# A fused attention and top-1 expert kernel: another order of the same units, and the fills of ones moved from VectorE to GpSimd

## The chip, the cores and the metric

The kernel runs on one core of one Trainium2 chip. The metric is the device time of one execution in microseconds; the time of a kernel is the median of several executions. A profile is one execution taken by the hardware profiler.

## The reference

The input x has 16 batches of 256 tokens with 128 features, 4096 tokens in all. The output is x plus two blocks that both read the layer-normalized x:

```python
xn = layernorm(x)                                  # over 128 features
# linear attention: 16 heads of 8, 64 random features each
q, k, v = xn @ Wq + bq, xn @ Wk + bk, xn @ Wv + bv
qp = relu(q . rw) + 1e-6;  kp = relu(k . rw) + 1e-6
attn = (qp @ (kp^T v)) / (qp @ sum_s(kp) + 1e-6) @ Wo + bo
# experts: 8, hidden width 512; each token goes to its best one
probs = softmax(xn @ wr + br);  gate = p1 / (p1 + p2)
ffn = gate * (gelu(xn @ w1[e] + b1[e]) @ w2[e] + b2[e])    # e = argmax
out = x + attn + ffn
```

All of it is in float32.

## The kernel before

The work is cut into small named units, and a string, `ORDER` (lines 66 to 116), lists them; line 814 runs through it and emits each. Line 137 fixes the order of TensorE (PE), VectorE (DVE), ScalarE (ACT) and SyncE (SP, which issues the plain DMAs) to that list. GpSimd (POOL) is not in line 137: its order is chosen when the program is built, from the same list and the dependences. Each engine works through its own instructions in order and waits by semaphores. A unit's name has its kind, then its number, then in some kinds the engine: `a` for ScalarE, `v` for VectorE.

**Head.** SP loads x in eight pieces of two batches, h = 0 to 7 (256 KB each, line 150), and two packs of constants. GpSimd and VectorE set up constants; among them VectorE fills with ones the upper half of every group of 32 columns of four tiles `va_c`, one for each chunk of four batches (line 192). These columns make the attention's denominator come out of the same products as its numerator. Then for every piece h:

- `st` (VectorE, line 285, two of them), `vr` (L294), `rs` (GpSimd, L299, the power -1/2), `nm` (L304): statistics; `xn` normalizes four tiles of 128 tokens (L311 on ScalarE or L313 on VectorE).
- `xd` (SP, L321) stores them in DRAM, in rows that the experts' gathers read.
- `tp` (PE, L327) turns the four tiles, `ev` copies them to xnT, `pv` (PE, L341) makes values and router logits; `lg` (L345) and `va` (L351) add the biases, `va` into the lower half of the groups of `va_c`.

For every chunk c: `c0` to `c6` (VectorE, L377 to L383) pick the best expert and the two best logits, `ct` (PE, L394) counts, `g0` to `g3` make the gate, `g4` (SP, L408) stores it beside the rows of xn. Then once: `ra` to `rl` (VectorE, L440 to L457) give every token a slot in 39 tiles of 128 tokens sorted by expert; `e0` to `e2` the expert of each tile; `hh` and `lo` (L475 to L477) compare, `iv0` and `iv1` (PE, L484, 16 products each) invert the map, and `s0` (L496) writes the token table that the gathers read.

**Attention.** For every pair of batches: `pj` (PE, L514) projects keys and queries, `pe` adds the biases (L521 on ScalarE, L523 on VectorE), `pq` (PE, L539) and `qf` (L548, or L555 and L557) make query features. For every batch, named in hexadecimal 0 to f: `pk` (PE, L581), `kf` (ACT, L592) key features, `kv` (PE, L607) keys by values, `mk`, `tk`, `nd` (L619, L630, L270), `at` (PE, L648), `a0` to `a5` (VectorE, L659 to L685) the quotient, `pw` (PE, L693) the output product, `ow` (L695) and `bo` (L697) the adds into x.

**Experts.** For every tile s = 00 to 38: `gx` (GpSimd, L716) gathers 128 rows from DRAM by an indirect DMA, `wl` (SP, L729) loads 578 KB of weights of the tile's expert, `fi` (PE, L734) turns, `xc` copies, `fu` (PE, L747) is the first product, `ht` (ACT, L754, four) the gelu, `gy` (L766) bias times gate, `fd` (PE, L775) the second product, `fy` (L783) the sum, `sc` (GpSimd, L790) scatters the 128 rows to DRAM by another indirect DMA. There are five weight buffers, three of which first hold tables of the routing (`iota_h`, `low` twice), seven buffers for gathered rows and six for results. A gather waits until the tile four before it has been copied out (line 723).

**End.** `ae` (GpSimd, L805) adds the rows of one chunk from DRAM into x by an accumulating DMA, after all scatters; `so` (SP, L700) stores the batches. PSUM is shared by three pools: two buffers for `pv`, `pj`, `pq`, `pk`; three for the small products; one for `ph` and the routing's.

Of the kernel before, what the change touches and what calls it, by code (L numbers as in the profile page):

```python
# [25 lines left out]
Q = 32  # L26
# [11 lines left out]
NCHUNK = B // CHUNK_B  # L38
# [25 lines left out]


ORDER = """
st00 st01 vr0 st10 st11 vr1 rs0 nm0 xn00v xn02v xn03a rs1 xn01v nm1 tp0 xn10v xn11v xn12v st20 xn13a tp1 st21
ev0a vr2 st30 st31 rs2 pv0 vr3 st40 pj0 nm2 xd1 xd0 va0 lg0 ev1a st41 vr4 rs3 xn20a rs4 nm3 xn22v st50 xn30v
xn31v st60 st51 pj1 vr5 xn32v xn33v xn23a pe00a nm4 xn21a pe01a pe11a tp2 pv1 st61 pe10v rs5 ev2a xn40a st70
xn43a nm5 lg1 xn41v xn50a va1 xn52v vr6 c00 tp3 pv2 va2 c01 ev3a xn51a lg2 rs6 xn42a pv3 nm6 tp4 va3 lg3 xn60a  # L70
pk0 xn63v st71 c02 ev4v vr7 c10 c03 xn53a xn61a xn62a c11 c12 tp5 rs7 c13 c14 kf00a kf01a ev5v nm7 tp6 xn70v
xn72a xn73a xn71v c04 c15 c05 c16 pv4 c06 g01 lg4 g00 g10 va4 pv5 ev6a tp7 va5 lg5 pv6 c20 bo1 g11 ev7a pv7 g21
ct0 c21 c22 c23 lg6 va6 g20 ct1 lg7 va7 pq00 c24 c30 c31 g31 c32 c25 g30 ct2 xd4 xd7 c26 c33 c34 qf000a qf000b
xd5 g02 qf001v c35 xd3 ct3 ra rb c36 rc g03 g12 g22 g13 kv0 rd re g23 pq01 rf mk00 e0 qf011a qf011b mk01 xd2 g33
g32 qf010v g40 g41 xd6 g42 rg tk0 e1 rh ri e2 rj g43 rk hh00 rl hh10 lo1 hh01 nd0a lo0 pk1 at0 hh11 kf10a kf11a
pj2 kv1 pe20a mk10 mk11 pe21a pk2 iv0 kf20a wl00 kf21a iv1 s0 a00 s1 bo3 wl01 tk1 pk3 nd1a kv2 mk20 at1 kf30a
kf31a gx00 fi00 gy00v s2 mk21 a01 pq10 xc00a qf100v kv3 fu00 ht000 ht001 wl02 qf101v bo4 gx01 gx02 mk30 ht002
ht003 mk31 gx03 wl03 tk2 fi01 xc01v pq11 nd2a qf110v a10 gy01v qf111v a20 fi02 fu01 xc02a ht010 wl04 ht011 ht012
gy02v ht013 fi03 tk3 fd00 fy00 fu02 xc03a ht020 a30 a40 gy03v a11 pj3 ht021 ht022 nd3a ht023 gx04 fi04 pe31a
xc04a fd01 gx05 pe30v fy01 a21 fu03 ht030 ht031 pk4 ht032 ht033 gx06 fd02 a50 gy04v bo7 bo2 gx07 fu04 fy02 wl05  # L80
bo0 fi05 wl06 ht040 ht041 xc05v pw0 ht042 ht043 gx08 kf40a fd03 sc00 ow0 kf41a fd04 fu05 gy05v fy03 fi06 xc06a
fi07 sc01 gx09 ht050 pk5 fy04 ht051 kv4 ht052 xc07a wl07 ht053 kf50a at2 fu06 kf51a pk6 fi08 ht060 ht061 wl08
ht062 bo6 gy06v a31 a02 mk40 mk41 xc08v ht063 fd05 kf60a fu07 fy05 gy07v tk4 gx10 gx11 kf61a wl09 sc02 fi09 fd06
ht070 ht071 ht072 ht073 a41 fu08 nd4a fi10 pq20 fy06 ht080 xc09a ht081 ht082 a51 ht083 fi11 pw1 fu09 ht090 ht091
gy08v xc10v ht092 wl10 xc11v qf200v ow1 fd07 ht093 sc03 sc04 sc06 gx12 gx13 qf201v fd08 fu10 fd09 wl11 wl12 fy07
fy08 gy09v gx14 a12 fy09 ht100 ht101 ht102 ht103 sc05 fi12 xc12a pq21 kv5 qf210v at3 a22 pj4 fu11 ht110 ht111
ht112 a32 a42 ht113 gx15 sc08 a52 a03 mk50 wl13 pw2 qf211v mk51 ow2 fi13 sc07 gy10v gy11v pe40a gy12v xc13v
pe41a fd10 fu12 ht120 ht121 fd11 fi14 fy10 bo5 fy11 a13 xc14a ht122 gx16 fi15 pq30 ht123 xc15v qf300v gy13v fd12
fu13 fy12 qf301v wl14 gy14v tk5 at4 gx17 ht130 a23 kv6 pq31 ht131 ht132 ht133 nd5a fu14 fi16 ht140 ht141 ht142
sc10 ht143 bo9 a04 mk60 fd13 sc09 a33 mk61 a43 tk6 a14 a24 wl15 fu15 nd6a ht150 wl16 ht151 xc16v gy15v qf311v  # L90
qf310v fd14 a53 fy13 ht152 gx18 ht153 a34 bo8 gy16v fy14 pk7 pw3 fi17 kf70a wl17 ow3 fu16 fi18 pj5 wl18 ht160
ht161 ht162 ht163 xc17v fu17 fd15 sc12 pe51a kf71a at5 a05 fy15 a15 ht170 xc18a kv7 a25 boa mk70 sc13 sc11 gy17v
ht171 ht172 pe50a gx19 ht173 gx20 wl19 pk8 fu18 fi19 ht180 mk71 gx21 gy18v xc19v a44 fi20 fd16 fd17 ht181 ht182
ht183 wl20 sc15 xc20a kf80a kf81a gy19v a54 fy16 fy17 fu19 pw4 gx22 sc14 gx23 fd18 ht190 ht191 ow4 ht192 ht193
fi21 wl21 fu20 fy18 wl22 fd19 a35 fi22 xc21v gy20v xc22v a45 fy19 pq40 ht200 ht201 qf400v ht202 at6 ht203 a06
qf401v kv8 fi23 fu21 fd20 xc23v a55 fy20 sc16 gx24 mk80 gy21v ht210 ht211 mk81 pq41 ht212 ht213 fu22 ht220 ht221
tk7 ht222 ht223 nd7a qf410v pw5 fd21 gx25 ow5 wl23 fy21 qf411v fi24 fu23 wl24 fi25 wl25 at7 pq50 ht230 sc17 gx26
sc18 gx27 ht231 ht232 ht233 xc24v bob a16 a07 a26 gy22v fu24 xc25a a36 a46 a17 tk8 wl26 gx28 sc21 fd22 fd23
qf500v a27 gy23v fy22 sc19 nd8a ht240 ht241 ht242 qf501v fy23 a56 wl27 gy24v ht243 fi26 xc26v fu25 fi27 fd24
pq51 xc27a ht250 fy24 qf511v gy25v ht251 ht252 ht253 fu26 wl28 fi28 ht260 xc28v qf510v fd25 pw6 ht261 ht262  # L100
ht263 gx29 sc20 fy25 ow6 fu27 gy26v a37 fd26 gx30 fy26 ht270 pk9 ht271 ht272 ht273 gx31 sc23 sc22 at8 kf90a gx32
kf91a gy27v a08 fu28 fi29 wl29 wl30 ht280 xc29a wl31 pka fi30 ht281 gx33 sc24 xc30v ht282 ht283 fi31 fd27 fd28
xc31a kfa0a kfa1a pj6 fu29 a47 pe60v fy27 kv9 kva ht290 pe61a ht291 pkb ht292 a18 ht293 fu30 ht300 wl32 gy28v
sc26 sc25 mk90 fy28 a28 gy29v mk91 mka0 ht301 ht302 mka1 fd29 ht303 a38 a48 a57 a58 pw7 pw8 ow7 fy29 ow8 fu31
fi32 xc32v fi33 tk9 fd30 kfb0a kfb1a ht310 ht311 gx34 sc28 ht312 ht313 nd9a xc33v wl33 fu32 ht320 ht321 ht322
ht323 wl34 at9 kvb gx35 sc27 gy30v fy30 mkb0 gy31v a09 pq60 tka a19 gy32v a29 fu33 ht330 ndaa mkb1 a39 fi34
xc34a fd31 boc fd32 fi35 qf600v ht331 ht332 fy31 ht333 xc35v fy32 qf601v gy33v wl35 fu34 ht340 ht341 a49 gx36
ata sc30 ht342 ht343 gy34v bod pq61 qf610v qf611v fu35 fi36 fd33 pj7 a0a ht350 gx37 xc36v ht351 ht352 fi37 wl36
ht353 gx38 sc29 fu36 pe70a xc37a ht360 ht361 gy35v pe71v fy33 ht362 ht363 fd34 fy34 fd35 fi38 wl37 fy35 gy36v
a1a fu37 wl38 ht370 pkc ht371 sc31 sc32 a2a xc38v a3a ht372 ht373 kfc0a a59 fd36 kfc1a fu38 sc35 ht380 bof ht381  # L110
ht382 a4a fd37 sc34 ht383 pkd pw9 boe a5a gy37v fy36 fy37 fd38 ow9 gy38v kfd0a tkb pwa kfd1a sc36 fy38 sc37 sc33
pke kvc owa mkc0 ndba mkc1 atb kvd kfe0a kfe1a sc38 mkd0 a0b a1b tkc pkf a2b mkd1 ndca atc a3b a4b kff0a a5b a0c
a1c a2c kve mke0 a3c kff1a pq70 tkd ndda pwb a4c mke1 ae1 ae2 ae0 ae3 atd kvf a5c qf700v so5 qf701v a0d pq71 so8
so0 owb a1d mkf0 a2d mkf1 sob qf710v qf711v a3d tke so3 so7 so2 a4d tkf pwc ndea a5d owc ndfa so9 so6 soa ate
a0e pwd owd a1e atf a2e a3e a0f so1 so4 soc a4e a1f a5e a2f pwe a3f a4f sod a5f owe soe pwf owf sof
"""


# [1 line left out]
def attn_plus_top1_moe(ctx: ExitStack, tc: tile.TileContext, x, cpack, wpack, out):  # L120
    nc = tc.nc
# [26 lines left out]
    for h in range(NH):  # L148
        c, i = h // 2, 2 * (h % 2)
# [39 lines left out]
    vaug = []  # L189
    for c in range(NCHUNK):  # L190
        va_c = const.tile([P, CT, NPAIR, Q], F32, name=f"va_{c}")
        nc.vector.memset(va_c[:, :, :, Q // 2 :], 1.0)  # L192
        vaug.append(va_c)
    ones = const.tile([P, P], F16, name="ones")
    nc.vector.memset(ones, 1.0)
# [63 lines left out]
    units = {}  # L259
# [8 lines left out]

    def copy(eng, out, in_):
        return nc.scalar.copy(out, in_) if eng == "a" else nc.vector.tensor_copy(out, in_)  # L270


    st, var, rstd, nmr, xns, xnT, pts, pvs = {}, {}, {}, {}, {}, {}, {}, {}
# [2 lines left out]
    def layernorm(h):  # L276
# [52 lines left out]
        def turned(eng):  # L329
            if c not in xnT:  # L330
                xnT[c] = xnp.tile([P, CT, P], F32, tag="xnT", name="xnT", bufs=4)
            copy(eng, xnT[c][:, g : g + 4, :], pts.pop(h))
# [31 lines left out]
    lg2 = route.tile([P, NT, E], F32, name="lg2")  # L364
# [203 lines left out]
    def batch(b):  # L568
# [63 lines left out]
        def turned(eng):  # L632
            nds[b] = work.tile([P, 2, 4, Q], F32, name="nd")
            copy(eng, nds[b].rearrange("p r q c -> p r (q c)"), pns[b])
# [75 lines left out]
    def expert_tile(s):  # L710
# [25 lines left out]
        def turned(eng):  # L736
            xTs[s] = work3.tile([P, P], F32, name="xT")
            copied[s] = copy(eng, xTs[s], pxs[s])
# [126 lines left out]
```

## Time and profile before

| | |
|---|---|
| median of 9 runs | 220.77 us (218.89 to 221.9) |
| the profiled execution | 222.7 us, its span 221.0 us |
| TensorE busy | 197.0 us (89%) |
| VectorE busy | 148.1 us (67%) |
| ScalarE busy | 111.1 us (50%) |
| GpSimd busy | 90.7 us (41%) |
| mean granted TensorE clock | 0.96 |

Times in the views are microseconds from the start of the span, those of single instructions means in ns. A view of waits names what ended an engine's idle time, by semaphore events; where the named engine had long been done it was another. The chain of waits goes back from the last instruction to what released it, step by step.

### The profile page before, as it was taken

The page shows a single profiled execution, that of the slowest core. Times are in us where ns is not written, and L with a number is a line of the kernel's source. Part 1 is how long each engine was busy: PE and PEld are TensorE (multiplying, and loading weights), DVE is VectorE, ACT ScalarE, POOL GpSimd, SP SyncE. Part 2 cuts the span into 40 slices and gives each one's busy share as a digit, 9 for nine tenths or more (in the row PEclk, how much of TensorE's full clock was granted, in tenths as well). Part 3 has the DMA queues.
Part 4 walks back from the last instruction along what each step waited for, and adds up shares of the span by engine and source line. Part 5 has one row for each costly group of instructions (what it writes and reads, how often), then busy time and mean ns, then how long its engine had stood idle before and what let it go on. Part 6 is the DMA issues. An engine that isn't in the chain of part 4 may idle for free.

```text
span 221.0 us, 5940 instructions
## 1 busy us (share of the span) xinstructions
PE 197.0 (89%) x2207; PEld 156.4 (71%) x2207; DVE 148.1 (67%) x437; ACT 111.1 (50%) x275; POOL 90.7 (41%) x104
## 2 busy tenths in 40 slices
PE   0299886994999999999999999999999999999834
PEld 0167764573787988978787989898788878876522
DVE  5999999921774534696863577975163796439973
ACT  6158747543255785424456724436648345854100
POOL 3353100024135747456353676377356153543000
PEclk9999999978599999999999999999999999999995
DMA  6940198795026857677574596489646463109982
GB/s 165 309 98 23 38 174 56 73 333 185 12 44 215 259 170 235 183 244 220 176 237 129 153 328 212 134 242 316 189 149 183 126 232 125 49 15 191 219 281 71
DMA packets 21870, 37.53 MB, mean 170 GB/s; under 512 B 6641, under 2 KB 14962, under 8 KB 21842
## 3 DMA queue, kind: packets, MB, share of 16 engines
q1 hardware_dynamic: 18770, 29.93, 46.1%
q0 software_dynamic: 3072, 7.23, 13.7%
q8 instruction: 17, 0.28, 0.5%
q14 instruction: 11, 0.09, 0.1%
HBM read 30.39 MB, written 6.77 MB: 168 GB/s over the span
## 4 chain that ended last, share of the span: by engine, by line
PE 60%; DVE 16%; DMA 13%; issue 5%; POOL 3%; ACT 1%; SPq 1%; POOLq 0%; DVEq 0%
PE ph L747 16%; PE py L775 15%; PE pq L539 6%; DMA x<-yd 6%; PE pp L514 4%; PE pk L581 4%; PE pkv L607 4%; PE pa L648 4%; DMA xg<-xd,token 3%; PE pw L693 3%; DMA w<-in_wpack_dram 3%; PE pt_x L734 2%; DVE va L351 2%; DVE va L192 2%; DVE xn L313 1%
## 5 line engine op out<-in xcount | busy, mean ns | idle before, releaser
L754 ACT ACTIVATE hT<-ph,w 128x128 f32<-128x128 f32 x156 | 45.9, 374 | 54.7 <-issue 40.2
L716 POOL DMA_INDIRECT xg<-xd,token x39 | 38.3, 982 | 65.0 <-DMA w<-in_wpack_dram 22.9
L790 POOL DMA_INDIRECT yd<-y,row x39 | 38.8, 994 | 28.1 <-DVE y L783 16.7
L747 PE MATMUL ph<-xT,w 128*128 128x128 f32 x312 | 43.7, 284 | 0.1
L747 PEld LDWEIGHTS ph<-xT,w 128*128 128x128 f32 x312 | 39.0, 195 | 6.2 <-issue 5.0
L775 PE MATMUL py<-w,hT 128*128 128x128 f32 x312 | 40.6, 277 | 0.1
L548 DVE TENSOR_SCALAR qpT<-pq 128x1024 f32<-128x1024 f32 x30 | 36.0, 1215 | 5.0 <-PE pq L539 5.0
L775 PEld LDWEIGHTS py<-w,hT 128*128 128x128 f32 x312 | 37.4, 192 | 1.7 <-issue 0.6
L592 ACT ACTIVATE kp<-pk 128x1024 f32<-128x1024 f32 x32 | 31.3, 1032 | 8.4 <-PE pk L581 6.6
L783 DVE SCALAR_TENSOR_TENSOR y<-py,xg,y 128x128 f32<-128x128 f32 x39 | 13.5, 346 | 12.5 <-PE py L775 12.2
L581 PE MATMUL pk<-cw,kT 32*128 32x256 f32 x256 | 20.4, 417 | 1.1 <-DVE qpT L548 0.9
L539 PE MATMUL pq<-qT,cw 32*128 32x256 f32 x256 | 20.2, 417 | 0.3 <-DVE lg L345 0.3
L648 PE MATMUL pa<-qpT,nd 128*32 128x256 f32 x256 | 17.7, 384 | 1.7 <-DVE x L695 1.1
L607 PE MATMUL pkv<-kp,va 128*32 128x129 f32 x512 | 18.4, 290 | 0.0
L607 PEld LDWEIGHTS pkv<-kp,va 128*32 128x32 f32 x512 | 14.9, 116 | 4.7 <-issue 3.1
L659 DVE STREAM_TRANSPOSE at<-pa 128x512 f32<-128x512 f32 x16 | 11.3, 704 | 9.6 <-PE pa L648 9.6
L619 DVE SCALAR_TENSOR_TENSOR kvm<-pkv,hmask 128x128 f32<-128x128 f32 x32 | 10.3, 337 | 8.6 <-PE pkv L607 8.6
L581 PEld LDWEIGHTS pk<-cw,kT 32*128 32x128 f32 x256 | 12.6, 192 | 4.6 <-issue 1.9
L539 PEld LDWEIGHTS pq<-qT,cw 32*128 32x128 f32 x256 | 12.7, 192 | 4.4 <-issue 3.1
L514 PE MATMUL pp<-xnT,cw 128*128 128x512 f32 x32 | 15.1, 599 | 0.1
L327 PE MATMUL pt<-ident,xn 128*128 128x128 f32 x32 | 5.7, 314 | 9.7 <-DVE xn L313 9.7
L299 POOL TENSOR_TENSOR rstd<-var,mhalf 128x4 f32<-128x4 f32 x8 | 8.1, 1017 | 14.3 <-DVE var L294 8.6
(108 smaller groups left out, 236.8 us busy)
## 6 DMA issues: line engine op xcount, KB each, us to landing
w<-in_wpack_dram SPq DMA_DIRECT2D x39, 578.0 KB, 3.8
x<-in_x_dram SPq DMA_DIRECT2D x8, 256.0 KB, 5.1
xd<-xn SPq DMA_DIRECT2D x8, 256.0 KB, 7.3
x<-yd POOLq DMA_DIRECT2D x4, 512.0 KB, 5.2
out_dram<-x SPq DMA_DIRECT2D x16, 128.0 KB, 2.2
xg<-xd,token POOLq DMA_INDIRECT x39, 3.6
yd<-y,row POOLq DMA_INDIRECT x39, 4.2
cw<-in_cpack_dram SPq DMA_DIRECT2D x1, 321.0 KB
```

The costliest lines, as they stand in the source:

```text
L514: nc.tensor.matmul(pps[k][:, i], cst(w), rhs, start=True, stop=True)
L539: nc.tensor.matmul(pqs[k, i][g // 2][:, g % 2, cols], cst("rwf")[rows, i * P : (i + 1) * P], qT[rows, cols], start=True, stop=True,)
L548: nc.vector.tensor_scalar(feats[k][:, i, 2 * g : 2 * g + 2, :], pqs[k, i][g], 0.0, EPS, ALU.max, ALU.add)
L581: nc.tensor.matmul(pks[b][g // 2][:, 2 * (g % 2) : 2 * (g % 2) + 2, t, :], kT[rows, 2 * (b % 2) + t, :], cst("rwf")[rows], start=True, sto ...
L592: nc.scalar.activation(o, i, AF.Relu)
L607: nc.tensor.matmul(pkvs[b][Q * q : Q * q + Q, r, :], vaug[c][:, 2 * bl + t, j, :], kp[:, t, j, :], start=(t == 0), stop=(t == 1),)
L648: nc.tensor.matmul(pas[b][Q * q : Q * q + Q, r, :], nds[b][:, r, q, :], feats[b // 2][:, j % 2, j // 2, cols], start=True, stop=True,)
L716: ins = nc.gpsimd.indirect_dma_start(out=xgs[s], out_offset=None, in_=xd[:, :], in_offset=bass.IndirectOffsetOnAxis(ap=rt["token"][:, s : ...
L747: nc.tensor.matmul(phs[s][:, i, :], ws[s][:, W1O + i * P : W1O + (i + 1) * P], xTs[s], start=True, stop=True)
L754: nc.scalar.activation(hTs[s][:, i, :], phs[s][:, i, :], AF.Gelu, bias=ws[s][:, B1O + i : B1O + i + 1])
L775: nc.tensor.matmul(pys[s], hTs[s][:, i, :], ws[s][:, W2O + i * P : W2O + (i + 1) * P], start=(i == 0), stop=(i == NC - 1),)
L790: ins = nc.gpsimd.indirect_dma_start(out=yd[:, :], out_offset=bass.IndirectOffsetOnAxis(ap=rt["row"][:, s : s + 1], axis=0), in_=ys[s], in ...
```

## The change

The same units are emitted in another order, over the whole list. The four fills of ones become four new units, `vm0` to `vm3`, on GpSimd, one for each chunk. Some units change engine: VectorE has 13 of the 32 `xn` where it had 16 and none of the eight `ev` where it had two, seven of the 16 `pe` (was four) and 20 of the 39 `xc` (was 22). In the list, the fills stand behind `rs6` (vm0), `gx02` (vm1), `sc11` (vm2) and before `gx35` (vm3). The stores of xn go `xd0 xd1 xd4 xd5 xd2 xd3 xd7 xd6` where they went `xd1 xd0 xd4 xd7 xd5 xd3 xd2`, then xd6 between the gates. Ahead of the first expert tile's `fi00`, TensorE has no `pk3`, `at0`, `at1`, which were there before. The four adds go `ae0 ae1 ae3 ae2` where they went `ae1 ae2 ae0 ae3`.

The code outside the list, and of the list the part up to the first expert tile and the end (before, then after):

```diff
@@ vaug
         va_c = const.tile([P, CT, NPAIR, Q], F32, name=f"va_{c}")
-        nc.vector.memset(va_c[:, :, :, Q // 2 :], 1.0)
         vaug.append(va_c)
@@ units
+    for c in range(NCHUNK):
+        units[f"vm{c}"] = lambda c=c: nc.gpsimd.memset(vaug[c][:, :, :, Q // 2 :], 1.0)
@@ ORDER
-st00 st01 vr0 st10 st11 vr1 rs0 nm0 xn00v xn02v xn03a rs1 xn01v nm1 tp0 xn10v xn11v xn12v st20 xn13a tp1 st21
-ev0a vr2 st30 st31 rs2 pv0 vr3 st40 pj0 nm2 xd1 xd0 va0 lg0 ev1a st41 vr4 rs3 xn20a rs4 nm3 xn22v st50 xn30v
-...
-ct0 c21 c22 c23 lg6 va6 g20 ct1 lg7 va7 pq00 c24 c30 c31 g31 c32 c25 g30 ct2 xd4 xd7 c26 c33 c34 qf000a qf000b
-xd5 g02 qf001v c35 xd3 ct3 ra rb c36 rc g03 g12 g22 g13 kv0 rd re g23 pq01 rf mk00 e0 qf011a qf011b mk01 xd2 g33
-g32 qf010v g40 g41 xd6 g42 rg tk0 e1 rh ri e2 rj g43 rk hh00 rl hh10 lo1 hh01 nd0a lo0 pk1 at0 hh11 kf10a kf11a
-pj2 kv1 pe20a mk10 mk11 pe21a pk2 iv0 kf20a wl00 kf21a iv1 s0 a00 s1 bo3 wl01 tk1 pk3 nd1a kv2 mk20 at1 kf30a
-kf31a gx00 fi00 gy00v s2 ...
-...
-ht382 a4a fd37 sc34 ht383 pkd pw9 boe a5a gy37v fy36 fy37 fd38 ow9 gy38v kfd0a tkb pwa kfd1a sc36 fy38 sc37 sc33
-pke kvc owa mkc0 ndba mkc1 atb kvd kfe0a kfe1a sc38 mkd0 a0b a1b tkc pkf a2b mkd1 ndca atc a3b a4b kff0a a5b a0c
-a1c a2c kve mke0 a3c kff1a pq70 tkd ndda pwb a4c mke1 ae1 ae2 ae0 ae3 atd ...
+st00 st01 vr0 st10 st11 vr1 rs0 nm0 xn00a xn02v xn03v xn01a tp0 rs1 nm1 xn10a st20 xn12v xn11v xn13a st21 ev0a
+st30 vr2 tp1 rs2 st31 st40 pv0 vr3 st41 pj0 rs3 st50 vr4 rs4 nm2 ev1a va0 lg0 xn20a xn21a st51 vr5 pv1 xn23a
+...
+c12 c30 c22 ct0 c13 g20 pk0 c31 c23 c14 g30 c15 c24 c32 c25 c33 ct1 c26 c34 c35 ct2 c16 c36 kf00a kf01a ct3 pk1 g02
+g01 ra g03 rb rc g11 g12 rd g22 g32 g13 g21 g23 re g40 kv0 rf rg e0 rh g33 g42 kf10a g31 ri rj e1 rk mk00 hh10
+rl hh00 kf11a g43 g41 hh01 e2 hh11 lo0 mk01 lo1 pk2 kf20a kf21a kv1 pq00 iv0 qf000a qf000b mk10 qf001v iv1 wl00
+tk0 pq01 s0 kv2 mk11 qf010v s1 tk1 pj2 gx00 gx01 nd0a qf011a qf011b fi00 ...
+...
+ht373 fd37 sc32 fy37 gy38v fu38 ht380 ht381 ht382 pw9 pkd ow9 a3a ht383 fd38 fy38 tkb kfd0a kvc kfd1a sc35 mkc0
+pke mkc1 bof ndba tkc atb a0b kfe0a a1b a4a kvd kfe1a ndca pkf sc36 mkd0 a5a a2b mkd1 a3b a4b kff0a pwa kff1a
+atc a5b owa a0c pwb pq70 tkd ndda sc37 a1c owb kve sc38 a2c ae0 ae1 a3c a4c qf700v qf701v atd a5c a0d mke0 pq71
+mke1 a1d qf710v a2d ae3 tke ae2 kvf pwc ...
```

## The prediction

> **What bounds the kernel now.** First the windows view, cut where the chain of waits changes engine; its columns are the stretch, its length, then busy us (and instructions) of PE, PE weight loads, VectorE (DVE), ScalarE (ACT), GpSimd (POOL), the granted clock, the DMA share and GB/s.
>
> ```profile
> 0.00:6.90 6.90, 0.00 (x0) 0.00 (x0) 4.62 (x17) 3.81 (x7) 1.76 (x14) 1.00 0.70 191
> 6.90:44.20 37.30, 30.75 (x278) 21.93 (x278) 35.59 (x133) 23.03 (x45) 8.10 (x8) 1.00 0.58 103
> 44.20:47.30 3.10, 3.10 (x38) 2.73 (x34) 0.06 (x2) 1.95 (x2) 0.00 (x0) 0.99 0.91 340
> 47.30:54.80 7.50, 4.67 (x66) 2.96 (x65) 1.64 (x6) 2.32 (x3) 4.11 (x4) 0.73 0.70 241
> 54.80:193.50 138.70, 138.47 (x1527) 115.20 (x1528) 87.51 (x235) 73.88 (x210) 71.99 (x73) 0.98 0.59 182
> 193.50:211.70 18.20, 16.56 (x282) 11.27 (x280) 13.36 (x34) 6.07 (x10) 4.69 (x5) 1.00 0.75 159
> 211.70:221.00 9.30, 3.46 (x24) 2.28 (x24) 5.36 (x16) 0.00 (x0) 0.00 (x0) 0.65 0.46 151
> ```
>
> The program has three parts. Up to 47.3 us VectorE sets the pace (35.59 of 37.30 us busy), until the token table exists. From the first expert tile (54.8) to the last (193.5) TensorE is busy for 138.47 of 138.70 us: no order can shorten that stretch except by its work. The tail of 27.5 us is a chain of scatter, add from DRAM, and the last batches. Next, the chain of waits in order of time (start, length, what), for the first part.
>
> ```profile
> 1.95 0.91 DVE va L192
> 3.03 0.91 DVE va L192
> 4.10 0.91 DVE va L192
> 5.17 0.91 DVE va L192
> 6.44 0.26 DVE one_et L209
> 7.00 0.67 DVE st L285 x2
> 7.95 1.05 POOL rstd L299
> ...
> 41.45 6.19 DMA w<-in_wpack_dram
> 47.76 6.92 DMA xg<-xd,token
> 54.81 0.45 PE pt_x L734
> ```
>
> The four fills stand at the head of the chain; at its foot the first gather takes 6.92 us from issue to landing, against a median of 3.6 us in the page's list of DMA issues. Third, the timeline of VectorE around the token table (the bracket is idle time before the row and what ended it).
>
> ```profile
> 40.55 1.22 DVE L477 TENSOR_TENSOR low<-iota_h,lo_h 128x2048 f16<-128x2048 f16 x1
> ...
> 42.08 1.22 DVE L477 TENSOR_TENSOR low<-iota_h,lo_h 128x2048 f16<-128x2048 f16 x1
> 43.21 0.48 DVE L476 TENSOR_TENSOR high<-high,tok_h 128x624 f16<-128x624 f16 x1
> 43.61 0.62 DVE L619 SCALAR_TENSOR_TENSOR kvm<-pkv,hmask 128x128 f32<-128x128 f32 x2
> 47.26 0.20 DVE L496 TENSOR_SCALAR token<-ps_tok 128x39 int32<-128x39 f32 x1 [3.04 <-PE ps_tok L484]
> ```
>
> VectorE has all inputs of the table's products ready at 43.6 and then waits 3.04 us for them.
>
> **The change, part by part.** *Start.* The four fills step by 1.07 us each. Without them the setup behind them (6.06 to 6.92, 0.86 us) would end at 2.8; but the first piece of x, issued at 0.74, lands after 2.8 us, at 3.5. So the first statistics start at 3.55 instead of 6.92: 3.4 us earlier. The later pieces land at about 4.2, 6.4, 7.8, 9.1, 10, 11.5 and 12.2 (issue plus the landings of 2.8 to 6.7 us that the row of L150 gives, between them by packet counts); worked through, the statistics want them at 4.4, 6.9, 8.1, 9.0, 9.8, 11.7 and 15.8, so they cost about 0.2 us.
>
> *VectorE up to the last compare (lo1).* From 6.92 to 43.61 it is 36.7 us. By start-to-start steps the new order takes out of this stretch three xn (0.26 each), two copies to xnT (0.60 each, now on ScalarE) and two qpT of pair 0 (1.13 and 1.09, now behind lo1): 4.2 us. 3.55 + 36.7 - 4.2 is 36.0. I add 1.0 us because the eight value products now press: on TensorE a transpose group (0.60) and a product group (1.1) follow each other at 1.7 us, and lg2 to lg7 each wait 0.1 to 0.7 us for them. lo1 ends at 37.0. ScalarE gains three xn and two copies, 2.5 us, and loses two kT/qT, 1.4 us; it is busy for 23.0 of 37.3 us there, so I cost this at nothing; without that cover it is 1.1 us.
>
> *The token table.* Before, its 32 products started 1.2 us after lo0 ended, behind key features on TensorE, and took 2.74 us. In the new order lo0 comes before lo1, so the first 16 run under lo1. What stands ahead of them on TensorE (pk1, kv0, pk2, kv1, pq00) waits on four kp of 0.97 us on ScalarE behind gate g03: 5.2 us from g03, while lo0 ends 6.3 us after it. So the token is ready 1.37 + 0.2 us after lo1: at 38.6 against 47.3, 8.7 us earlier.
>
> *The gather.* This gain isn't all kept. Weight loads wl00 to wl04 go out at 40.27, 41.45, 43.3, 46.0 and 47.3, and the packets of the first four gathers, issued from 47.76 on, begin only at 51.0, when the 640 weight packets are nearly through. In the new order e2, which allows wl00, stands behind hh01, only 4.6 us ahead of the token instead of 8.2: wl00 at 35.2, wl04 at 38.6. Bounds for the first transpose fi00 (54.8 before): 43.0, where TensorE gets there and a gather of 3.6 us has landed; 46.0, the token plus the 7.4 us seen between 47.3 and 54.7; 49.6, the 14.4 us from the first weight load to the landed gather, kept whole. Weights set the delay, so I look between the last two; as the five loads are now asked for closer together, I take 47.5, 7.3 us earlier. TensorE idles there about 4 us (2.84 before).
>
> The stores of xn and gate are moved on SP's queue ahead of the weights: the last gate is issued at about 32.4, 6.2 us before the token (10 us before in the old order), so I cost them at nothing; if one store took over 6 us, the gathers would wait for it.
>
> *The middle.* TensorE has 36 units up to fi00 where it had 39: pk3 (1.08) and at0, at1 (0.95 each), 3.0 us, now lie behind it. The middle is 138.7 + 3.0 = 141.7 us if TensorE stays fed. Along the new order a tile's first product comes at least 6.8 us of TensorE work after the weight buffer is free (also 6.8 before, loads take 3.8), and a gather's tile at least 9.6 us after the buffer's earlier use, as before. So fd38 ends at 189.2 instead of 193.5. GpSimd isn't among the engines whose order the list fixes (line 137), and indeed the trace has eight gathers before its first scatter where the old list has nine: where the moved gathers and scatters stand I can't read from the list; with TensorE fed either way I cost their move at nothing, with one to two stalls as the other end (third rival).
>
> *The tail.* The scatter sc38 starts 0.66 us after fd38 and the adds last 14.4 us from their first issue, unchanged. VectorE has a4, a5 of batch a and one bias add more behind fy38, 1.0 us, but is idle for 4.8 of 17.8 us there. The add for batches c to f is now third of four; the owc add waited 1.47 us for it. Bounds -1.5 and +1.0; I take 0, as VectorE's own work ends where that wait ended.
>
> *The fills on GpSimd.* Its 128x128 memset takes 0.20 and its 128x1 memset 0.10 us, so 128x1024 is 0.9 us by their slope (estimate). Beside other work: nothing. In front of the first rstd: all four fill 2.4 to 6.1, and rstd, ready at 4.6, is up to 1.5 us late.
>
> *Sum:* -7.3 + 3.0 + 0 = -4.3 us. The profiled execution took 222.7 us (span 221.0 and 1.7 around it), so 218.4; the median of the runs is 1.93 us below that execution: 216.5.
>
> **Rivals.** *Gathers aren't held* (0.18). If the gathers' packets get their turn among the weights', fi00 comes at 43.2: -11.6 + 3.0 = -8.6, 212.2 us. Against it stands the 3.2 us between issue (47.76) and first packet (51.0); for it, that the next gather, issued at 55.83 without weights, had packets at 57. The Trainium skill, DMA: Bandwidth & Descriptors, section Queues, rings and completion order, says that each DMA engine takes queues in turn, packet by packet. By that rule this rival would be right, and the trace does not agree.
>
> *The fills stop VectorE* (0.14). If each fill on GpSimd holds VectorE's accesses for its whole time, 4 x 0.9 = 3.6 us comes back on the path: -0.7, 220.1 us, no change. For it: VectorE is 95% busy there, so any hold counts. Against: during the rstd of 9.0 to 10.0 us, three xn took 0.34 us, their usual time; but rstd has only four elements a partition. The Trainium skill, SBUF — State Buffer, section SBUF: two separate sides, speaks against this change: the two engines share a port pair as an exclusive lock, held for the whole instruction. The xn rows show no such hold.
>
> *A scatter stands before a gather* (0.13; slower). GpSimd works in order; the longest wait of a scatter for its rows was 5.01 us. The least time from a gather's issue to its tile was 6.6 us, 3.0 more than a landing; a gather behind such a scatter starves TensorE for 2.0 us, and the clock adds at least 1.7: the windows show it halved for two stretches between 47 and 61 us, 3.4 and 6.8 us long, around TensorE's idle time. One stall leaves -0.6; from two on the change loses: -4.3 + 7.4 = +3.1, 223.9 us. Against it: 138.47 of 138.70.
>
> **How the numbers follow.** My forecast has 0.55, with its own range 214 to 219.5 (fi00 between 45 and 49.6, fills up to 1.5, tail -1.5 to +1.0). The range 212 to 221 takes in the first two rivals and leaves out the third and the ends. A measurement of this kernel can tell about 0.5%, 1.1 us. Faster by more: 0.53 of my own 0.55, 0.18, and 0.04 of the second rival, 0.75. Within: 0.02 + 0.08 + 0.01 = 0.11. Slower: 0.02 + 0.12 = 0.14.
>
> **What would show it.** First st row at 3.5; token (L496) near 38.6 with under 1.6 us since the last low row; fi00 near 47.5 with first gather packets behind the weights; TensorE over 98% busy from there for about 142 us. Wrong if va fills precede the first rstd with VectorE standing still, if TensorE shows gaps with gathers as releaser in the middle, or if fi00 comes after 51.8, where the head gains no more than the moved work costs.

## The result, and the profile after

| | before | after |
|---|---|---|
| median | 220.98 us (62 runs) | 214.56 us (20 runs, 212.85 to 216.84) |
| ratio | | 0.9715, 95% interval 0.9692 to 0.9737 |
| profiled execution, its span | 222.7, 221.0 us | 214.52, 212.7 us |
| first transpose of an expert tile (fi00) starts | 54.81 | 46.29 |
| last second product (fd38) ends | 193.50 | 186.22 |

The windows view of the changed kernel, cut at the same events; its columns are those of the prediction's first view.

```profile
0.00:6.90 6.90, 0.00 (x0) 0.00 (x0) 3.68 (x19) 3.81 (x7) 6.30 (x19) 1.00 0.69 193
6.90:37.50 30.60, 28.76 (x256) 21.64 (x256) 28.49 (x117) 22.63 (x46) 7.04 (x8) 1.00 0.67 120
37.50:39.10 1.60, 1.60 (x21) 1.46 (x18) 1.43 (x4) 0.40 (x1) 0.00 (x0) 1.00 0.84 306
39.10:46.30 7.20, 5.92 (x57) 3.35 (x55) 2.36 (x7) 2.55 (x3) 4.12 (x4) 0.76 0.92 327
46.30:186.20 139.90, 139.38 (x1575) 115.45 (x1575) 89.51 (x234) 75.71 (x214) 71.89 (x73) 1.00 0.58 181
186.20:203.20 17.00, 16.46 (x279) 10.82 (x277) 14.10 (x37) 6.06 (x9) 4.66 (x5) 1.00 0.74 152
203.20:212.70 9.50, 3.34 (x30) 1.98 (x28) 5.41 (x17) 0.37 (x1) 0.00 (x0) 0.88 0.56 185
```

The span is 8.3 us shorter: 8.5 in front of the first expert tile (54.8 to 46.3), 1.2 lost again in the middle (138.7 to 139.9), 1.0 gained in the tail (27.5 to 26.5). The medians moved by 6.4 us, less than the two profiled executions, because the one of before is among the slower ones of its kernel, 1.7 us above the median of 220.98. The chain of waits, first part:

```profile
2.07 0.89 POOL va L273
2.96 0.28 POOL tri masks.py:66
3.24 2.71 POOL va L273 x3
5.95 1.02 POOL rstd L302
...
34.99 1.15 DVE low L480
36.18 2.88 PE ps_tok L487 x32
39.08 0.20 DVE token L499
39.28 0.28 DVE kvm L622
39.59 6.66 DMA xg<-xd,token
46.27 0.29 DVE y L769
```

Two things to see. The fills still head the chain, only on another engine: all four stand in front of the first `rstd`, although the list has them much later; GpSimd's order is chosen by the build. And the gather takes 6.66 us, almost as long as before (6.92), only 8.2 us earlier. VectorE's timeline shows the rest of the start:

```profile
3.48 0.76 DVE L288 BATCH_NORM_STATS2 st<-x 128x6 f32<-128x256 f32 x2 [0.22 <-DMA x<-in_x_dram]
4.27 0.79 DVE L297 TENSOR_SCALAR var<-st 128x4 f32<-128x4 f32 x1
4.35 0.75 DVE L288 BATCH_NORM_STATS2 st<-x 128x6 f32<-128x256 f32 x2
5.14 0.83 DVE L297 TENSOR_SCALAR var<-st 128x4 f32<-128x4 f32 x1
7.00 0.16 DVE L307 SCALAR_TENSOR_TENSOR nmr<-st,rstd 128x4 f32<-128x4 f32 x1 [1.02 <-POOL rstd L302]
...
36.31 1.21 DVE L480 TENSOR_TENSOR low<-iota_h,lo_h 128x2048 f16<-128x2048 f16 x1
39.08 0.20 DVE L499 TENSOR_SCALAR token<-ps_tok 128x39 int32<-128x39 f32 x1 [0.17 <-PE ps_tok L487]
```

The first statistics start at 3.48, when x has landed. The two `var` rows take 0.79 and 0.83 us where they took 0.17 before, and the second ends with the last fill (5.97; the chain has the fills end at 5.95). The token is 1.56 us behind the end of the last `low`, where it was 3.96 (43.30 to 47.26); VectorE's own wait ahead of it went from 3.04 to 0.17.

### The profile page after: what moved, and what is told of

Read it like the earlier page. It is cut to its first block, busy times and chain, and to the rows that moved or that the text cites. A ratio compares the mean times of both kernels' runs of the same rounds, so it can differ in the third digit from the quotient of the medians.

```text
span 212.7 us, 5951 instructions
## 1 busy us (share of the span) xinstructions
PE 195.5 (92%) x2207; PEld 154.7 (73%) x2207; DVE 145.0 (68%) x429; ACT 111.5 (52%) x279; POOL 94.0 (44%) x108
## 4 chain that ended last, share of the span: by engine, by line
PE 75%; DVE 14%; DMA 3%; POOL 3%; ACT 2%; issue 1%; POOLq 0%; ACTq 0%
PE ph L750 17%; PE py L778 17%; PE pk L584 7%; PE pp L517 6%; PE pq L542 6%; PE pa L651 5%; PE pkv L610 5%; DMA xg<-xd,token 3%; PE pw L696 3%; PE pt_x L737 2%; DVE qpT L551 2%; PE pv L344 2%; POOL va L273 2%; PE pt L330 2%; DVE va L354 1%; PE pt_kv L633 1%
## 5 line engine op out<-in xcount | busy, mean ns | idle before, releaser
L757 ACT ACTIVATE hT<-ph,w 128x128 f32<-128x128 f32 x156 | 46.4, 373 | 45.0 <-issue 30.7
L750 PE MATMUL ph<-xT,w 128*128 128x128 f32 x312 | 42.9, 281 | 0.2 <-ACT hT L757 0.2
L750 PEld LDWEIGHTS ph<-xT,w 128*128 128x128 f32 x312 | 38.3, 192 | 6.3 <-issue 4.7
L778 PE MATMUL py<-w,hT 128*128 128x128 f32 x312 | 41.2, 277 | 0.0
L595 ACT ACTIVATE kp<-pk 128x1024 f32<-128x1024 f32 x32 | 31.5, 1024 | 13.7 <-PE pk L584 13.3
L786 DVE SCALAR_TENSOR_TENSOR y<-py,xg,y 128x128 f32<-128x128 f32 x39 | 13.2, 344 | 15.8 <-PE py L778 15.7
L584 PE MATMUL pk<-cw,kT 32*128 32x256 f32 x256 | 21.0, 402 | 0.3
L651 PE MATMUL pa<-qpT,nd 128*32 128x256 f32 x256 | 17.2, 383 | 0.3 <-DVE kvm L622 0.3
L610 PEld LDWEIGHTS pkv<-kp,va 128*32 128x32 f32 x512 | 13.9, 113 | 4.1 <-issue 2.8
L517 PE MATMUL pp<-xnT,cw 128*128 128x512 f32 x32 | 15.6, 609 | 0.2 <-ACT qT L524 0.2
L270 ACT COPY nd<-pt_kv 128x256 f32<-128x256 f32 x16 | 6.0, 376 | 13.8 <-PE pt_kv L633 13.8
```

Of the source, the lines that this page charges most:

```text
L517: nc.tensor.matmul(pps[k][:, i], cst(w), rhs, start=True, stop=True)
L584: nc.tensor.matmul(pks[b][g // 2][:, 2 * (g % 2) : 2 * (g % 2) + 2, t, :], kT[rows, 2 * (b % 2) + t, :], cst("rwf")[rows], start=True, sto ...
L595: nc.scalar.activation(o, i, AF.Relu)
L610: nc.tensor.matmul(pkvs[b][Q * q : Q * q + Q, r, :], vaug[c][:, 2 * bl + t, j, :], kp[:, t, j, :], start=(t == 0), stop=(t == 1),)
L651: nc.tensor.matmul(pas[b][Q * q : Q * q + Q, r, :], nds[b][:, r, q, :], feats[b // 2][:, j % 2, j // 2, cols], start=True, stop=True,)
L750: nc.tensor.matmul(phs[s][:, i, :], ws[s][:, W1O + i * P : W1O + (i + 1) * P], xTs[s], start=True, stop=True)
```

## The experiments

Each is the changed kernel with one edit, unless told otherwise. The first four ran side by side (the kernel before: 220.71 us there).

**The fills alone.** The kernel before, with its old list, and only the fills on GpSimd:

```diff
-        nc.vector.memset(va_c[:, :, :, Q // 2 :], 1.0)
+        nc.gpsimd.memset(va_c[:, :, :, Q // 2 :], 1.0)
```

> The kernel before with its old order; only the four fills of ones go to GpSimd, at the same place of the setup. Path theory (the fills cost what they keep the first statistics from): first statistics at 3.5 us instead of 6.9, first rstd held to about 6.0 by the fills in front of it, so the head is 2.0 us earlier (7.9 to 6.0) and the total 2 us less, 219. Hold theory (each fill on GpSimd stops VectorE for its whole time): the 3.6 us come back beside VectorE's work, no change, 221; the order then carries the whole gain.

Measured: 219.22 us, ratio 0.9894 (0.9846 to 0.9942). Statistics start at 3.59, and the last compare (`high`) ends at 42.30 instead of 43.69, yet the token is ready at 47.23 (before: 47.26). TensorE's timeline shows where the gain went, first before, then with the fills moved:

```profile
37.82 1.15 PE L581 MATMUL pk<-cw,kT 32*128 32x256 f32 x16 [0.94 <-DVE qpT L548]
38.89 1.07 PE L648 MATMUL pa<-qpT,nd 128*32 128x256 f32 x16
40.07 1.98 PE L514 MATMUL pp<-xnT,cw 128*128 128x512 f32 x4
```

```profile
36.43 2.09 PE L581 MATMUL pk<-cw,kT 32*128 32x256 f32 x16 [0.94 <-DVE qpT L548]
38.45 1.68 PE L648 MATMUL pa<-qpT,nd 128*32 128x256 f32 x16
40.06 1.98 PE L514 MATMUL pp<-xnT,cw 128*128 128x512 f32 x4
```

The products of key features (`pk`) come 1.39 us earlier, but they and `pa` take 3.63 us up to `pp` instead of 2.25: here a half-clock stretch lies over them (granted clock 0.51 from 36.3 to 39.8). From `pp` on TensorE runs alike in both, and the table's products start at 44.47 and 44.48. So 1.39 us of the gain at the start reach TensorE and are lost there at half clock; whether they would have reached the token without it, no run shows. The time that the path theory gave (219) came out, but not by its path: the token is no earlier. This run also shows the old list's middle without a half-clock stretch (the windows view from fi00 to the end of fd38):

```profile
54.15:190.08 135.93, 135.73 (x1527) 113.40 (x1528) 87.45 (x235) 73.72 (x210) 71.89 (x73) 1.00 0.60 185
```

**The order alone.** The new list, the fills on VectorE as before:

```diff
+        nc.vector.memset(va_c[:, :, :, Q // 2 :], 1.0)
...
-        units[f"vm{c}"] = lambda c=c: nc.gpsimd.memset(vaug[c][:, :, :, Q // 2 :], 1.0)
+        units[f"vm{c}"] = lambda: None
```

> The changed kernel with the four fills back on VectorE in the setup. Path theory: the first rstd falls back by 2.0 us, to 7.9, and nearly all of it arrives at the token table and the end: 216.5, so order 4.4 and fills 2.0 of the 6.4 us. Hold theory: taking the fills off GpSimd frees VectorE as much as they cost it: 214.6, as the changed kernel.

Measured: 216.49 us, ratio 0.9798 (0.9759 to 0.9837); token 41.14, fi00 48.49, middle 139.96. The order is worth 4.2 us of the median and the move of the fills 2 us more; taken the other way round, the fills alone gave 1.5 and the order 4.7 on top. With the new order the fills bring the token 2.06 us forward (41.14 to 39.08), about as much as they bring the first `rstd` forward (7.95 to 5.92).

**The fills behind the last statistics.** The same fills on GpSimd, made to come after the last `rstd`:

```diff
-        units[f"vm{c}"] = lambda c=c: nc.gpsimd.memset(vaug[c][:, :, :, Q // 2 :], 1.0)
+        units[f"vm{c}"] = lambda c=c: after(
+            nc.gpsimd.memset(vaug[c][:, :, :, Q // 2 :], 1.0), powers[NH - 1], "statistics first"
+        )
...
-            nc.gpsimd.tensor_tensor(rstd[h], ...)
+            powers[h] = nc.gpsimd.tensor_tensor(rstd[h], ...)
```

with `vm0` to `vm3` behind `rs7` in the list.

> The changed kernel with the four fills on GpSimd behind the last rstd (near 20 us) instead of ahead of the first. Path theory: the first rstd starts at 4.5 instead of 5.9, the first transposes 1.3 us earlier; pieces of x land in time to about 10 us, so 0.5 to 1.3 us less: 213.3 to 214. Hold theory: VectorE is as busy at 20 us as at the start, and the variance rows of 0.79 and 0.83 us seen beside the early fills (0.17 elsewhere) move there: some of its operations take 0.6 to 0.9 us longer, up to 3.6 in all, and the total is 214.5 to 217.

Measured: 214.35 us, ratio 0.9703 (0.9664 to 0.9743). VectorE's timeline:

```profile
4.32 0.17 DVE L300 TENSOR_SCALAR var<-st 128x4 f32<-128x4 f32 x1
...
5.19 0.17 DVE L300 TENSOR_SCALAR var<-st 128x4 f32<-128x4 f32 x1
...
20.75 0.52 DVE L319 TENSOR_SCALAR xn<-x,rstd,nmr 128x128 f32<-128x128 f32 x1
```

With no fill beside them the `var` rows are back at 0.17, so their length in the changed kernel came from the fills. Two `xn` run while the four fills stand on GpSimd (19.36 to 23.15). The view of tiles has the shortest, middle and longest of all `xn` on VectorE and of the fills:

```profile
L319 DVE TENSOR_SCALAR xn<-x,rstd,nmr x13: 325/341/520, 5.9 to 21.0; 128x128 f32<-128x128 f32 x13
L275 POOL MEMSET va<- x4: 945/952/1111, 19.4 to 22.2; 128x1024 f32 x4
```

The first of the two is the long one: it ends 0.08 us after the second fill (20.24 and 0.95), and the third fill, beside it, is the one that took 1.11. Both repeat in the two later runs with late fills (`xn` 0.50 and 0.52, a fill of 1.12 and 1.11); no other `xn` of VectorE in any run took over 0.35. So a fill and an `xn` do hold each other up, by 0.2 us here, and VectorE starts its next instruction on time (21.02, 0.26 behind, as elsewhere). `rstd` starts at 4.58 instead of 5.92, the token at 38.04 instead of 39.08, and the profiled execution is 1.36 us shorter (213.16 to 214.52). In the medians (214.35 and 214.56) this gain can't be told from none.

**Weights behind the gather.** Four of the first five weight loads wait until the first gather has landed:

```diff
+    gathers = []
...
             ins = nc.gpsimd.indirect_dma_start(...)
+            gathers.append(ins)
...
-            nc.sync.dma_start(out=ws[s], in_=...)
+            ins = nc.sync.dma_start(out=ws[s], in_=...)
+            if s in (1, 2, 3, 4):
+                after(ins, gathers[0], "the first rows come first")
```

> The changed kernel with the weight loads of tiles 1 to 4 made to wait until the first gather has landed. If the first gathers wait behind weight packets, they land about 3.6 us after their issue at 39.6, by 43.2; TensorE itself gets to the first transpose at 45.0, so it starts 1.3 us earlier, and the weights of tiles 1 to 4, asked for at 43.2, land by 46 to 54, each ahead of its use: 213.3. If the gathers wait for something else (the rows' own stores, descriptors), the first transpose stays at 46.3 and the total at 214.6, or above it where weights come late, up to 217.

Measured: 212.5 us, ratio 0.962 (0.9588 to 0.9653): faster than both kernels, and its interval lies below that of the changed kernel. GpSimd and TensorE in its timeline:

```profile
39.06 1.24 POOL L720 DMA_INDIRECT xg<-xd,token  x1 [19.25 <-DVE kvm L622]
...
42.64 1.88 PE L517 MATMUL pp<-xnT,cw 128*128 128x512 f32 x4
44.36 0.27 PE L741 MATMUL pt_x<-ident,xg 128*128 128x128 f32 x1
```

The first gather's packets begin 1.95 us after its issue (39.06 to 41.01); in the changed kernel it is 4.56 us (39.59 to 44.15), and 230 weight packets begin after GpSimd's row ends and before the gather's first; with weights held none does. The gather has landed by 41.85, when SP goes on with the held loads, and TensorE reaches `pt_x` at 44.36 without idling: its own work is now what ends last. So the hold is the weights', as the forecast said, and not the gather's own cost.

**The rest ran twice, on two other chips**, where every execution, the kernel before's too (248.26 and 247.0 us), took 26 to 27 us longer. The time is lost between fi00 and fd38 (163.7 us in the second run with `at0` put back, 139.9 in the changed kernel); its cause wasn't found. The changed kernel itself did not run there. So only the ratios, the heads and the tails of these runs are used, and a ratio is set beside the changed kernel's 0.9715 with that reserve.

*Both edits together* (late fills, weights held).

> The changed kernel with both: fills behind the last rstd, and the weight loads of tiles 1 to 4 behind the first landed gather. If the two act on different waits (the start of the statistics, and the gather), they add: first transpose 1.0 to 1.4 us ahead of the 44.4 of the held version, total 211 to 211.8. If the held version already waits for TensorE's own work in the head, which starts with the first rstd too, the sum is the same; if instead something else (landing of x, ScalarE) has become the bound of the head, the late fills add nothing: 212.5.

> The same kernel as late_and_held, once more. The theory that the start of the first gathers is set by weight packets, and that both gains lie on one path: the fills behind the last rstd bring s0 to about 38.1 us, the first gather lands about 2.8 us behind its issue, and TensorE's own work up to fi00 (about 43.4 to 44) is what ends last: 211 to 212 us, 0.5 to 1.5 us below weights_held (212.5). The rival (fills' place is worth nothing in the end): 212.5, as weights_held.

Measured: 240.34 and 240.5 us, ratios 0.9696 (0.9598 to 0.9795) and 0.9694 (0.9613 to 0.9775). `rstd` starts at 4.53 and 4.64 as expected, but the token comes at 38.71 in both, no earlier than with weights held alone (38.56). fi00 does come earlier, 43.10 against 44.36, and the reason is the clock, as the windows view shows for the stretch ahead of it, first with weights held alone, then with both edits (first run; the second has a clock of 1.00 there too):

```profile
38.70:43.10 4.40, 4.40 (x53) 3.04 (x53) 2.44 (x8) 2.55 (x3) 3.17 (x3) 0.61 0.18 45
```

```profile
38.70:43.10 4.40, 4.40 (x56) 2.56 (x55) 2.27 (x7) 2.55 (x3) 3.17 (x3) 1.00 0.17 37
```

At the first second product (fd00) nothing is left of it: 49.65 and 50.26 against 49.79. I expected the two gains to add up; these runs show no sum. In the second run waits of TensorE for VectorE (0.4) and ScalarE (0.5 and 0.8) stand between the two; with weights held alone it is one of 0.4.

*The transfers at once* (gathers and scatters listed where each can first go, the rest as changed; this isn't the old list's order either): the list has `s1 gx00 gx01 gx02 gx03 ...` and each later `gx` behind the copy it waits for, each `sc` behind its `fy`.

> The changed kernel with the gathers listed right behind the copy that frees them and the scatters right behind their rows, instead of planned apart. Forecast: GpSimd's order isn't fixed by the list and TensorE stays fed either way: no change, 214 to 215. Third rival (a gather behind a scatter starves TensorE): a gap of 2 us or more in the middle with a gather as releaser, 216 or more.

> The same kernel as transfers_at_once, once more. The theory that what the gathers wait for is the weight packets, which are there in any case: 214 to 215 us, as the changed kernel (214.6), since the order of the other transfers hardly moves the first gather's landing (fi00 45 to 46.5). The rival that planning the indirect transfers apart is where the gain lies: 216 us or more.

Measured: 242.5 and 242.35 us, ratios 0.9813 (0.9743 to 0.9884) and 0.9786 (0.9694 to 0.9877). fi00 is no later than in the changed kernel (44.89 and 45.70 against 46.29). GpSimd's order hardly moves: in both, seven gathers come before the first scatter, and only neighbours change places after that. The ratios lie 0.7% to 1% above the changed kernel's 0.9715, but from other chips and with an interval that still reaches it in one of two runs. So the head's gain isn't from planning the transfers apart; whether that planning brings 1.5 to 2 us elsewhere stays open.

*The adds earlier*: the four adds right behind `sc38` and `a2c`, in the order `ae1 ae2 ae0 ae3`, and `owb` behind them, as its place was before; the rest of the tail as changed.

```diff
-sc37 a1c owb kve sc38 a2c ae0 ae1 a3c a4c qf700v qf701v atd a5c a0d mke0 ... a2d ae3 tke ae2 kvf
+sc37 a1c kve sc38 a2c ae1 ae2 ae0 ae3 a3c a4c qf700v qf701v atd a5c a0d owb mke0 ... a2d tke kvf
```

> The changed kernel with the four adds from DRAM in the old order, ae1 ae2 ae0 ae3, and owb behind a0d as it was. If the tail's 1.0 us came from the add for batches c to f being third, owc waits again for the last add and the tail is 27 us or more: up to 1 us slower, 215 to 215.6. If VectorE's own work sets the tail, no change: 214.6.

> The same kernel as adds_old, once more: the old order of the last adds and scatters, the rest as changed. The theory that the tail's 1.0 us comes from the order of the adds: 215 to 216 us, with fd38's end to owc about 18 us instead of 16.9. If the last product waits for the last add behind them, 219 to 222 us, with that wait ahead of owc in the trace. The rival that the tail's difference is chance: 214.6 us.

Measured: 249.92 and 249.01 us, ratios 1.0123 (1.0034 to 1.0213) and 1.0072 (1.0024 to 1.0119). VectorE's timeline of the second run:

```profile
228.85 0.42 DVE L698 TENSOR_TENSOR x<-pw,x 128x256 f32<-128x256 f32 x1 [5.06 <-DMA x<-yd]
```

`owb` adds into rows of the chunk that `ae2` adds into from DRAM. Issued behind `ae2`, it waits 5.06 us for that DMA to land, and all of VectorE's tail stands behind it: from the end of fd38 to the end of `owf` it is 31.1 and 30.7 us, against 23.8 in each of the six other runs on those chips. This isn't the old tail, where `owb` came so late that the add had landed; the runs show that the place of `owb` ahead of `ae2` is worth some 7 us in the new list (5.06 of it the wait itself), not where the 1.0 us between the two kernels come from.

*One product put back*: `at0` ahead of `fi00`. The text on record names pk3 too; the edit moves `at0` alone.

```diff
-qf011a qf011b fi00 s2 mk20 gy00v mk21 at0 pe21v
+qf011a qf011b at0 fi00 s2 mk20 gy00v mk21 pe21v
```

> The changed kernel with one unit, at0 (1.0 us of TensorE), put back ahead of the first transpose of an expert tile, into the 1.3 us in which TensorE waits for the first gather. If the end is the first transpose plus the work behind it, 1.0 us less: 213.6. If the first gelu (its table load) sets the pace of the first tiles, nothing: 214.6.

> The same kernel as at0_back, once more: pk3, at0 in front of fi00 as in the kernel before, the rest as changed. The theory of the prediction (TensorE idles ahead of fi00, so work put there is free): the idle 1.27 us ahead of fi00 is filled and the middle gets shorter by as much, 213.3 to 214 us. The rival that this work would run ahead of fi00 only in part and push fi00 later: 214.6 to 215.5 us.

Measured: 243.23 and 239.81 us, ratios 0.9805 (0.9722 to 0.9889) and 0.9757 (0.9683 to 0.983): no gain over 0.9715. TensorE in the second run:

```profile
44.06 1.07 PE L651 MATMUL pa<-qpT,nd 128*32 128x256 f32 x16
47.05 0.30 PE L737 MATMUL pt_x<-ident,xg 128*128 128x128 f32 x1 [1.93 <-DVE kvm L622]
47.71 2.08 PE L750 MATMUL ph<-xT,w 128*128 128x128 f32 x8 [0.35 <-ACT xT L270]
```

`pa` runs at 44.06, where TensorE would have idled. But the product behind `pt_x` now takes 2.08 us instead of 1.16: in these runs the half-clock stretch lies at 47.6 to 51.0, behind the idle time, where in the changed kernel it lies at 39.7 to 43.1, ahead of it. And `pt_x` now waits for a `kvm` of VectorE that stands behind `y`, the first reader of the gathered rows: it starts 0.65 us behind that `y` (46.40), where the changed kernel has 0.02. From token to fd00 it is 13.2 and 13.3 us with `at0` ahead, and 13.2 to 13.5 in the two runs with the adds earlier, which leave `at0` where the change put it. The work hidden in the gap was paid back in this wait and at half clock.

## Why the prediction was right, and where it was off

- **Start.** First statistics forecast at 3.55, measured 3.48. The fills were costed at nothing beside other work, with up to 1.5 us of late `rstd` if they came first. They came first, and `rstd` is 1.34 us late (5.92 against 4.58 in the run with late fills); 1.04 of it reaches the token. The prediction had named fills ahead of the first `rstd`, with VectorE standing still, as a sign of being wrong, and it came in part: VectorE idles 1.02 us for that `rstd`, 0.30 with late fills. The late `rstd` should have been in the sum: nothing in the list could keep the fills behind the first `rstd` on an engine whose order the list doesn't fix.
- **Token.** Forecast 38.6, measured 39.1; lo1 ends at 37.52 against 37.0, and the token is 1.56 us behind it, as forecast (1.57). The order alone gives 41.14.
- **Gather.** The mechanism held: the first gather waits behind weight packets (run with weights held). Its size was off: I took fi00 at 47.5, between the bounds 46.0 and 49.6, and it came at 46.29, 0.3 us above the bound that keeps the old 7.4 us from token to tile (now 7.21). Asking for the weights closer together did lengthen the wait for the gather's first packet (4.56 against 3.24), but not the time from issue to landing (6.66 against 6.92). This term gave 1.2 us more than forecast.
- **Middle.** Forecast +3.0 us, measured +1.2. The work moved in was not too small: against the old list's middle without half clock (135.93) it is 139.9 - 135.9 = 4.0 us, of which 0.3 is more time in which TensorE wasn't busy (0.52 against 0.20). What I missed is that the profiled execution of before carries 2.8 us of half clock in its middle (138.70 - 135.93; its row of the windows view has 0.98), which isn't work and so need not come back. Whether that is the 1.93 us by which this execution stands above the median isn't shown: nine of the eleven runs of before beside the first experiments have a mean clock of 0.962 to 0.967, much like its own 0.962, so the half clock may well be in them too.
- **Tail.** Forecast 0 with bounds -1.5 and +1.0, measured -1.0. It repeats: from the end of fd38 to the end of `owf` the changed kernel and the first three kernels with its list (order alone, fills late, weights held) all have 23.36 to 23.38 us; those with the old list have 24.66 and 24.16. `owc` no longer waits for a DMA (1.47 us before). Part of before's extra is clock: its last row of the windows view has 0.65, the changed kernel's 0.88. With the fills alone the half clock comes only 0.4 us before the end of `owf`, and 0.8 us of extra is left. How much of that is the adds' order is not separated.
- **Sum.** -4.3 forecast against -8.3 between the spans and -6.2 from the 220.77 that the forecast started from: head 1.2, middle 1.8 and tail 1.0 better than the terms. Of these 4.0 us some 1.9 don't show in the medians, because the profiled execution of before stood that much above 220.77. All three errors lie on the same side, and 214.56 is near the lower end of the forecast's own range (214 to 219.5): the direction and the waits were right, the size was short by 1.9 us.

The rivals. *Gathers aren't held*: false. By the Trainium skill, DMA: Bandwidth & Descriptors, section Queues, rings and completion order, as I applied it (turns after each packet of the trace), the gather's packets would have started some 2 us after the issue, as they do with weights held; 4.56 us and 230 weight packets say otherwise. That section also lets one turn last for a packet of some 9 to 17 descriptors; if the trace's rows are descriptors, 230 over 16 engines are 14 each, and the rule would fit. No run here tells which. *The fills stop VectorE*: the hold exists, and my sentence that the trace shows none was too wide. Two `var` rows grew by 0.62 and 0.66 us, ending with a fill, but VectorE would have waited for `rstd` then anyway, so they cost nothing themselves, and the statistics behind the first still started at 4.35; with late fills one `xn` grew by 0.18. Few of VectorE's instructions are held, so the 3.6 us of this rival didn't come. The Trainium skill, SBUF — State Buffer, section SBUF: two separate sides, gives the lock on the shared ports only for some kinds of VectorE instruction, which my short version left out; these three rows agree with a lock held to the fill's end. *A scatter before a gather*: not seen. These are all of TensorE's waits from fi00 to fd38 in the changed kernel, by the view of waits (total, times, longest):

```profile
PE pt_x L737 <- DMA xg<-xd,token: 1.3, 1, 1.3
PE pa L651 <- DVE kvm L622: 0.3, 1, 0.3
PE ph L750 <- ACT hT L757: 0.2, 1, 0.2
```

The first is the wait ahead of fi00 itself; behind it no gather and no scatter holds TensorE up.

## What to carry to other kernels

A gain at the start has to be followed to the instruction that everything waits for: moving the fills brought the token 2.06 us forward with the new order and 0.03 with the old one, where TensorE lost it again in a half-clock stretch. When a small transfer that everything waits for is issued among large ones that have slack, make the large ones wait for it: that beat the whole reordering's result by 2 us with an edit of a few lines. And look at the granted clock stage by stage before summing terms against a profiled execution, or putting a loss down to the order: 2.8 us of the old middle was half clock, not work.

## What the runs showed of the hardware

- GpSimd fills 128x1024 floats in 0.95 to 0.97 us, hardly longer than VectorE's 0.91; the slope from its small fills had given 0.9.
- A VectorE TENSOR_SCALAR on 128x4 floats took 0.79 and 0.83 us beside a GpSimd fill instead of 0.17, and one on 128x128 (`xn`) 0.50 to 0.52 instead of 0.34, with the fill beside it at 1.11 to 1.12. A merged row of two `xn` hides this (0.61 against 0.60); the single ones show it.
- A half-clock stretch is 3.4 or 6.8 us long (those that run into the end of an execution aside), and where it falls decides its price: from 39.7 on, ahead of a wait for the gather, it left TensorE 1.27 us idle all the same in the changed kernel, while 6.8 us from 54.05 on cost the kernel before 2.8 us of its middle.
